# A graph layer on one core: where the weights' stores are issued, border differences in one pass, earlier limits, and a table of choices between streams

## The chip, the core and the metric

The kernel runs on one core of one Trainium2 chip. The metric is the device time of one execution in microseconds (us). The core has five engines that work side by side and each take their own list of instructions strictly in order: TensorE (PE in the profile, its weight loads PEld), VectorE (DVE), ScalarE (ACT), GpSimd (POOL) and SyncE (SP), which here only issues DMAs. Data is moved between HBM and the on-chip memory (SBUF) by DMA; matmuls write to PSUM[...].

## The reference

32 graphs of 512 nodes with 256 channels each. In float32:

```python
h = jnp.maximum(_layernorm(x, axis=-1), 0.0)
xc = jnp.transpose(h, (0, 2, 1))
c = jax.nn.relu(_bn(_conv1d(xc, conv1_w, 0), ...))
c = _bn(_conv1d(c, conv2_w, 8), ...)                 # 17 taps along the nodes
x_conv = jnp.transpose(jax.nn.relu(c + xc), (0, 2, 1))
s = h @ w_se.T + b_se                                 # 3 numbers for each node
dist = sq[:, :, None] + sq[:, None, :] - 2.0 * jnp.einsum('bnd,bmd->bnm', s, s)
A = jnp.exp(-dist) * adj
msg = jax.nn.relu(h @ w_msg.T + b_msg)
x_nmp = jnp.einsum('bnm,bmd->bnd', A, msg)
x_in = jnp.concatenate([x_conv, x_nmp], axis=-1)
# a GRU cell with x_in as its input and h as its state: gates r and z, then n
out = x + (1.0 - z) * n + z * h
```

## The kernel before

The kernel is a program that writes out, once and at build time, one fixed list of instructions for each engine. It holds a planner: `Engine` and `on_pe` keep a clock for each engine and for each buffer, with a cost for each kind of instruction, and the order of the lists follows from these clocks. On the chip nothing is decided; only semaphores hold an instruction until its inputs and buffers are there.

The work is in five streams (lines 1771 to 1777), each a Python generator that emits a few PE instructions and then says when it can go on: `begins` (normalise a graph and turn it, so that channels lie on partitions), `rows` (first convolution, conv1, into `h1`), `conv` (the 17 taps), `graphs` (messages, the adjacency kernel A with exponential and mask, and the gather A times msg) and `gates` (the GRU cell). The loop at line 1819 takes, among the streams that are ready, the one whose `clock` is furthest behind. If none is ready it lets 0.25 us pass in its own clock; until the gates begin, every fourth such turn puts one filler transpose on PE (`keep_warm`, lines 267 to 272). After each turn `fill` gives VectorE and ScalarE work from the background: sums, norms, weights, operands.

The 17-tap convolution is computed with two nested short-convolution schemes of five products each, 25 products in place of the taps' number. It runs in seven groups of positions (`STARTS`, line 36; group 0 has 116 columns, the others 135 or 136).

- `weights_first` (717) makes the 25 sets of weights once, in group 0. VectorE makes combinations of the taps: `g` of `wraw` (128x1536) on the outer level, `gg` of `g` (128x512) on the inner. ScalarE scales them into the tiles `w`, of which there is a ring of six, and line 754 stores each to DRAM (`wd`) from ScalarE's own queue. From group 1 on SyncE loads them again, and `third_weight` (782) stores a third tile to `wd` from GpSimd's queue during group 1. `prepare_some` (967) lets a step of this go only while ScalarE's clock is at most `BUSY` = 0.5 us ahead of PE's.
- `operands` (663) makes the other side of the products from `h1`: on the outer level 18 phases become `x1` with six, on the inner level `fives` (562) makes five operands with two phases each from an `x1`. A difference that reaches past the last phase takes the next column of an early phase instead, so it is done in two instructions: `sub` (572) does the first phase or phases in one and the border one in another.
- `norm` (479) and `norm_some` (508) are the layer norm: statistics on VectorE, `rstd` by a power on GpSimd, scaling on ScalarE. `norm_ahead` (1687) lets the norm of graph b begin in the background when the messages of graph b - 4 have been issued (`told >= b - 3`).
- GpSimd's queue also stores the turned inputs (`hd`), the gathered sums (`nd`), the untransposed inputs (`xd`), the convolution's results (`cd`) and, with accumulation, the output.

Of the kernel before, what the change touches and what calls it, by code (L numbers as in the profile page):

```python
# [10 lines left out]
ALU = mybir.AluOpType  # L11
# [20 lines left out]
G = 4  # L32
# [18 lines left out]
def kernel(  # L51
# [43 lines left out]
    now = 0.0  # L95
    LAG = 0.17
    BUSY = 0.5
# [20 lines left out]
    def done(*tiles):  # L118
        at = 0.0
        for a in tiles:  # L120
            for k, end in met(a.tensor.name, region(a)):
                if k[4]:
                    at = max(at, end + HAND)
        return at
# [24 lines left out]
    class Pool:  # L149
# [18 lines left out]
        def over(self):  # L168
            return max(map(released, self.made)) + HAND
# [75 lines left out]
    dve, act = Engine("DVE", nc.vector, 0.066, 0.00106, 0.085), Engine("ACT", nc.scalar, 0.05, 0.00087, 0.12)  # L245
    pool, sp = Engine("POOL", nc.gpsimd, 1.1, 0.0003, 0.0), Engine("SP", nc.sync, 0.0, 0.0, 0.0)
# [20 lines left out]
    def keep_warm(n):  # L267

        nonlocal now
        for _ in range(n):  # L270
            now += 0.11
            nc.tensor.transpose(unused[:, :P], ident, ident)
# [11 lines left out]
    def later(t, f):  # L284
        LATER.append((t, f))
        LATER.sort(key=lambda e: e[0])
# [221 lines left out]
    def norm_some(b):  # L508

        if now < NORM_AT[b] or act.free > now + BUSY:  # L510
            return False
        NORM_AT[b] = next(NORMS[b], NORM_AT[b])
        if NORMS[b].gi_frame is None:
            del NORMS[b]
        return True
# [46 lines left out]
    def fives(src, n, rv, new, again=None):  # L562

        flat = src.rearrange("p q e -> p (q e)")

        def get(k, some=n):
            return src[:, k : k + 3 * some - 2 : 3, :]  # L570

        def sub(dst, a, b):
            some = n if a < 3 else n - 1
            dve.tensor_tensor(dst[:, :some, :], get(a, some), get(b, some), op=ALU.subtract)
            if a > 2:
                at = [src[:, 3 * n - 3 + b, :], flat[:, (b - 3) * rv + 1 : (b - 2) * rv + 1]]
                dve.tensor_tensor(
                    dst[:, some, :], flat[:, (a - 3) * rv + 1 : (a - 2) * rv + 1], at[b > 2],
                    op=ALU.subtract,
                )  # L580

        def less2(dst, a, b):
            dve.scalar_tensor_tensor(dst, a, -2.0, b, op0=ALU.mult, op1=ALU.add)

        d1 = new()
        sub(d1, 3, 1)
        yield d1
        t = new()
        sub(t, 2, 0)
        yield None  # L590
        less2(t, t, d1)
        yield t
        if not again:
            t = new()
        sub(t, 4, 2)
        yield None
        less2(t, d1, t)
        yield t
        f2 = new()
        sub(f2, 3, 2)  # L600
        yield None
        t = new()
        sub(t, 2, 1)
        yield None
        less2(t, t, f2)
        yield t
        less2(f2, get(1), f2)
        yield f2
# [54 lines left out]
    def operands(g):  # L663

        rv = sizes(g)[3]
        h = h1[:, : Q * rv].rearrange("p (q e) -> p q e", q=Q)
        if g == 0:
            more = iter([cv, prep] * 2)
            firsts = fives(h, 6, rv, lambda: x1_of(next(more), rv), again=True)
        else:  # L670
            firsts = fives_alone(h, 6, rv, x1_of(cv, rv))
        for x1 in firsts:
            yield None
            if x1 is not None:
                yield from fives(x1, 2, rv, lambda: phases("x2", 2, rv, 6))
# [11 lines left out]
    WD = [dram.tile([P, 3, ND, D], F32, name=f"wd{n}") for n in range(25)]  # L687

    def taps_of(get, new, inplace):

        t = new()
        dve.scalar_tensor_tensor(t, get(1), 2.0, get(0), op0=ALU.mult, op1=ALU.add)
        dve.scalar_tensor_tensor(t, get(2), 4.0, t, op0=ALU.mult, op1=ALU.add)
        yield t
        yield get(0)
        yield get(2)
        t = new()
        dve.tensor_tensor(t, get(0), get(1), op=ALU.subtract)
        dve.tensor_tensor(t, t, get(2), op=ALU.add)
        yield t  # L700
        s = t if inplace else new()
        dve.scalar_tensor_tensor(s, get(1), 2.0, t, op0=ALU.mult, op1=ALU.add)
        yield s

    WS, W_AT = [], []
# [6 lines left out]
    def new_w():  # L712
        nonlocal taken
        taken += 1
        return cv.tile([P, ND, D], F32, name="w", bufs=RING)

    def weights_first():


        outer = [  # L720
            taps_of(
                lambda k, i=i: wraw[:, i, :, :, k, :],
                lambda i=i: prep.tile([P, 2, 3, D], F32, name=f"g{i}", bufs=1),
                True,
            )
            for i in range(ND)
        ]
        for j1 in ORDER:
            g = []
            for o in outer:  # L730
                g.append(next(o))
                yield 0.0
            inner = [
                taps_of(
                    lambda k, i=i: g[i][:, :, k, :],
                    lambda i=i: prep.tile([P, 2, D], F32, name=f"gg{i}", bufs=2),
                    False,
                )
                for i in range(ND)
            ]  # L740
            for j2 in ORDER:
                gg = []
                for i in range(ND):
                    gg.append(next(inner[i]))
                    yield 0.0
                yield dve.free + 0.1
                W_BASE.append(taken)
                w = [new_w(), new_w()]
                for k in range(2):
                    for i in range(ND):  # L750
                        act.activation(
                            w[k][:, i, :], gg[i][:, k, :], AF.Copy, scale=GSCALE[j1] * GSCALE[j2]
                        )
                    act.dma_start(WD[len(WS)][:, k], w[k])
                WS.append(w)
                W_AT.append(act.free + LAG)
                yield 0.0
# [181 lines left out]
    at_product = 0  # L939
# [10 lines left out]
    def operand_some():  # L950
# [12 lines left out]
        return True  # L963

    prepare, prepare_at = weights_first(), 26.0

    def prepare_some():
        nonlocal prepare_at
        if len(WS) >= 25 or len(WS) >= at_product + 3 or now < prepare_at or act.free > now + BUSY:
            return False  # L970
        prepare_at = next(prepare)
        return True
# [713 lines left out]

    def norm_ahead():
        for b in list(NORMS)[:2]:
            if (b < G or told >= b - 3) and norm_some(b):
                return True  # L1690
        return False

# [22 lines left out]
    def fill():  # L1715
        while LATER and LATER[0][0] <= now:
            LATER.pop(0)[1]()
        if EVAC:
            evacuate()
        for b in (gating, gating + 1):  # L1720
            if b in HB:
                load_conv(b)
                if dve.free < now + 1.5:
                    residual(b)
                    data_sums(b)
        while dve.free < now + 1.5 and background():
            pass
# [50 lines left out]
    clock = {name: at for name, (_, _, at) in streams.items()}  # L1778
    ready = {name: 0.0 for name in streams}
    hold = {name: None for name in streams}  # L1780


    unused, waits = acc.tile([P, N], F32, name="ps_acc"), 0
    now = max(5.0, done(ident))
    keep_warm(16)
    load(0)
    while 0 in NORMS:
# [8 lines left out]
        op=ALU.add,  # L1796
# [22 lines left out]
    while streams:  # L1819
        names = [k for k in streams if hold[k] is None or hold[k]()]  # L1820
        able = [k for k in names if ready[k] <= now]
        if not able:
            now += 0.25
            assert now < 1e4
            waits += 1
            if waits % 4 == 3 and not HB:
                keep_warm(1)
            fill()
            continue
        name = min(able, key=lambda k: clock[k])  # L1830
        waits = 0
        hold[name], began = None, now
        got = next(streams[name][0], None)
        if got is None:
            del streams[name]
        elif callable(got):
            hold[name] = got
        else:
            ready[name] = got
        if name == "conv":  # L1840

            clock[name] = at_product / 25 - max(0, at_product - 25 * (NG - 1)) * 0.004
        elif got is not None:
            clock[name] += (now - began) / streams[name][1]
        fill()
# [49 lines left out]
```

## Time and profile before

| | us |
|---|---|
| median of three runs | 2040.22 |
| the three runs | 2039.55 to 2042.61 |
| the profiled execution | 2034.87 |
| span of its instructions | 2033.1 |

The mean granted clock of TensorE in this execution was 0.993 of full speed. The costliest lines of the page's groups, PE's, are the products of the convolution and of the gates: here the name of the tile written, then those read, count, busy time, mean of one in ns, and the idle time before with its releaser.

```profile
L259 PE MATMUL ps_c<-xd,w 128*128 128x135 f32 (+1 forms) x2304 | 291.1, 279 | 4.3 <-ACT ps_c L241 3.5
L259 PE MATMUL ps_c<-x,w 128*128 128x135 f32 (+2 forms) x2032 | 269.6, 282 | 3.4 <-ACT n L241 1.1
L259 PE MATMUL ps_g<-at,msg 128*128 128x512 f32 x512 | 227.8, 593 | 1.3 <-DVE shift L241 1.2
```

All instructions are issued through a few helpers, so most lines of the profile are L259 (matmul), L265 (transpose by TensorE), L272 (filler), L241 (VectorE, ScalarE, GpSimd) and L228 (DMA); the tile names tell the groups apart. `ps_c` are the convolution's banks, `ps_g` those of begins, rows and graphs, `ps_acc` those of the gates and fillers. A float32 matmul stands in the trace as two records.

### The profile page before, as it was taken

The numbers are of one execution on the slowest core, as the hardware profiler recorded it, in microseconds if no ns is written. First come the engines' busy times: TensorE is split into PE (matmuls) and PEld (weight loads), VectorE is DVE, ScalarE is ACT, GpSimd is POOL, SyncE is SP. The second block draws the span as 40 slices with busy tenths as digits, with TensorE's granted clock in tenths as the row PEclk, the third lists the DMA queues.
The fourth block names the chain that finished last, engine by engine and source line by source line (L and its number), as shares of the span: only waits on it lengthen the run. The fifth ranks groups of instructions, "written<-read, shape, count | busy, mean of one in ns | idle before, by whom it ended". The sixth has DMA issues, their size and how long they took to land. (4 is left out here: it accounts for less than half of the span.)

```text
span 2033.1 us, 28623 instructions
## 1 busy us (share of the span) xinstructions
PE 1979.4 (97%) x9707; PEld 1448.2 (71%) x9707; DVE 1512.4 (74%) x2816; ACT 876.4 (43%) x1755; POOL 450.9 (22%) x578
## 2 busy tenths in 40 slices
PE   8999999999999999999999999999999999999998
PEld 4778666767777767787678776667777578776774
DVE  5789688969997467897688885668894688766443
ACT  5554563435534444433454234444343543325221
POOL 2100021322311233121232122231122311113232
PEclk9999999999999999999999999999999999999999
DMA  7555587898897879888897888788877866665664
GB/s 262 173 177 182 216 231 214 220 229 221 208 230 193 192 163 189 200 207 232 174 224 188 205 197 190 163 188 202 220 183 185 202 170 156 166 155 104 111 99 34
DMA packets 581377, 378.92 MB, mean 186 GB/s; under 512 B 457664, under 2 KB 475488, under 8 KB 580096
## 3 DMA queue, kind: packets, MB, share of 16 engines
q1 hardware_dynamic: 419760, 279.15, 49.4%
q0 software_dynamic: 153184, 84.70, 24.5%
q10 hardware_dynamic: 8288, 13.24, 1.8%
q8 instruction: 77, 1.26, 0.3%
q14 instruction: 68, 0.56, 0.1%
HBM read 278.94 MB, written 114.56 MB: 194 GB/s over the span
## 5 line engine op out<-in xcount | busy, mean ns | idle before, releaser
L228 POOL DMA_DIRECT2D out_dram<-o_sb x252 | 276.2, 1731 | 629.5 <-DVE o_sb L241 564.8
L259 PEld LDWEIGHTS ps_c<-xd,w 128*128 128x128 f32 x2304 | 285.1, 190 | 46.9 <-ACT ps_c L241 30.2
L259 PEld LDWEIGHTS ps_c<-x,w 128*128 128x128 f32 x2032 | 259.6, 194 | 58.1 <-issue 34.6
L259 PE MATMUL ps_c<-xd,w 128*128 128x135 f32 (+1 forms) x2304 | 291.1, 279 | 4.3 <-ACT ps_c L241 3.5
L259 PE MATMUL ps_c<-x,w 128*128 128x135 f32 (+2 forms) x2032 | 269.6, 282 | 3.4 <-ACT n L241 1.1
L259 PE MATMUL ps_g<-at,msg 128*128 128x512 f32 x512 | 227.8, 593 | 1.3 <-DVE shift L241 1.2
L259 PE MATMUL ps_acc<-xconv,wih 128*128 128x512 f32 (+2 forms) x532 | 210.9, 494 | 4.3 <-DVE shift L241 2.2
L259 PE MATMUL ps_acc<-hTb,whh 128*128 128x512 f32 (+2 forms) x532 | 211.0, 496 | 2.0 <-ACT r L241 2.0
L259 PE MATMUL ps_acc<-xnb,wih 128*128 128x512 f32 (+2 forms) x532 | 209.3, 495 | 3.7 <-DVE ps_acc L241 3.4
L241 DVE TENSOR_TENSOR ps_acc<-ps_acc,r 128x256 f32<-128x256 f32 x120 | 51.6, 430 | 212.0 <-PE ps_acc L259 200.1
L259 PE MATMUL ps_acc<-t,wsum 128*128 128x256 f32 x720 | 177.1, 382 | 5.3 <-ACT ps_acc L241 2.8
L259 PEld LDWEIGHTS ps_g<-at,msg 128*128 128x128 f32 x512 | 95.3, 190 | 106.6 <-issue 100.0
L259 PEld LDWEIGHTS ps_acc<-t,wsum 128*128 128x128 f32 x720 | 135.7, 191 | 41.8 <-issue 17.8
L259 PEld LDWEIGHTS ps_acc<-xconv,wih 128*128 128x128 f32 x532 | 97.5, 190 | 49.3 <-issue 35.4
L259 PEld LDWEIGHTS ps_acc<-xnb,wih 128*128 128x128 f32 x532 | 96.2, 190 | 44.9 <-issue 29.2
L241 DVE TENSOR_TENSOR x<-x 128x272 f32<-128x272 f32 (+5 forms) x280 | 127.6, 498 | 0.3
L259 PEld LDWEIGHTS ps_acc<-hTb,whh 128*128 128x128 f32 x532 | 95.9, 191 | 44.2 <-issue 31.9
L259 PE MATMUL ps_g<-wmsg,hTg 128*128 128x259 f32 x496 | 124.6, 382 | 0.0
L259 PE MATMUL ps_acc<-t,wih 128*128 128x256 f32 x480 | 123.2, 379 | 0.0
L241 DVE TENSOR_TENSOR msg<-ps_g,bmsg 128x256 f32<-128x256 f32 x128 | 53.4, 418 | 93.8 <-PE ps_g L259 93.8
L259 PE MATMUL ps_g<-hT,w 128*128 128x512 f32 (+8 forms) x296 | 118.8, 548 | 3.8 <-DMA hT<-hd 3.5
L241 ACT ACTIVATE h<-ps_g,bn_shift,bn_scale 128x252 f32<-128x252 f32 (+8 forms) x212 | 86.6, 482 | 58.0 <-PE ps_g L259 57.4
(157 smaller groups left out, 3241.9 us busy)
## 6 DMA issues: line engine op xcount, KB each, us to landing
w<-wd SPq DMA_DIRECT2D x414, 256.0 KB, 3.7
m_sb<-in_adj_dram SPq DMA_DIRECT2D x384, 64.0 KB, 3.5
hT<-hd SPq DMA_DIRECT2D x33, 512.0 KB, 3.8
hd<-hT POOLq DMA_DIRECT2D x32, 512.0 KB, 5.8
hTb<-hd SPq DMA_DIRECT2D x32, 512.0 KB, 4.8
xnb<-nd SPq DMA_DIRECT2D x64, 256.0 KB, 3.4
out_dram<-o_sb POOLq DMA_DIRECT2D x252, 64.0 KB, 4.6
hTg<-hd SPq DMA_DIRECT2D x31, 512.0 KB, 4.7
```

What stands on the lines that cost most here:

```text
L228: self.engine.dma_start(dst, src, **more)
L241: getattr(self.engine, op)(*tiles, **more)
L259: nc.tensor.matmul(ps, lhsT, rhs, **more)
```

## The change

There are five edits.

1. `store_w`: the 50 stores of the first-made weights go to GpSimd's queue instead of ScalarE's, and are put off by 0.3 us in the planner's clock.
2. `sub` in `fives`, for two phases and a difference that reaches past the last one: one instruction instead of two, with `over`, a view of two rows whose second lies before the first in memory (phase k, then phase k - 3 one column on).
3. `prepare_some` lets ScalarE's clock be 1.0 us ahead of PE's instead of 0.5.
4. `norm_ahead` lets a norm begin one graph sooner (`told >= b - 4`).
5. `OTHERS`: the planner counts the turns at which more than one stream is ready; at 26 of these it takes the second in the order of the clocks, at one the third.

```diff
+            if n == 2 and a > 2:
+                dve.tensor_tensor(dst, over(a), get(b) if b < 3 else over(b), op=ALU.subtract)
+                return
...
+        def over(k):
+            e = src[:, k, :]
+            return bass.AP(e.tensor, e.offset, [e.ap[0], (1 - 3 * rv, 2), (1, rv)])
...
+    def store_w(dst, src):
+        later(act.free + 0.3, lambda: pool.dma_start(dst, src))
...
-                    act.dma_start(WD[len(WS)][:, k], w[k])
+                    store_w(WD[len(WS)][:, k], w[k])
...
-        if len(WS) >= 25 or len(WS) >= at_product + 3 or now < prepare_at or act.free > now + BUSY:
+        if len(WS) >= 25 or len(WS) >= at_product + 3 or now < prepare_at or act.free > now + 1.0:
...
-            if (b < G or told >= b - 3) and norm_some(b):
+            if (b < G or told >= b - 4) and norm_some(b):
...
+    OTHERS = {
+        6: 1, 41: 1, 259: 1, 374: 1, 430: 1, 443: 1, 547: 1, 953: 1, 979: 1, 1020: 2,
+        1022: 1, 1182: 1, 1202: 1, 1260: 1, 1291: 1, 1471: 1, 1636: 1, 1670: 1, 1744: 1,
+        1745: 1, 1837: 1, 2031: 1, 2149: 1, 2232: 1, 2391: 1, 2604: 1, 2610: 1,
+    }
+    choices = 0
...
-        name = min(able, key=lambda k: clock[k])
+        able.sort(key=lambda k: clock[k])
+        choices += len(able) > 1
+        name = able[min(OTHERS.get(choices, 0), len(able) - 1)] if len(able) > 1 else able[0]
```

Since all lists come from one planner, each edit moves instructions everywhere after the place where it first acts. The instruction lists of the two programs have the same matmuls and transposes of data. They differ in 15 fillers fewer (45 to 30), 50 stores moved from ScalarE to GpSimd, and 210 small subtractions that become 105.

## The prediction

> **What bounds the kernel now.** I read the page first: busy shares, then the slices.
>
> ```profile
> PE 1979.4 (97%) x9707; PEld 1448.2 (71%) x9707; DVE 1512.4 (74%) x2816; ACT 876.4 (43%) x1755; POOL 450.9 (22%) x578
> PE   8999999999999999999999999999999999999998
> PEclk9999999999999999999999999999999999999999
> ```
>
> The reader is to see that TensorE has work at all times and that no other engine comes near it. The instruction lists of both programs hold the same matmuls; the only difference on PE is 45 against 30 of the filler transposes (`keep_warm`). So the time can move only by what PE loses. The busy times by stage say where that is (start up to the first product, the rest of group 0, the long middle, the gates at the end):
>
> ```profile
> core 0: us, PE busy (x) PEld busy (x) DVE busy (x) ACT busy (x) POOL busy (x), PEclk, DMA share, GB/s
> 0.00:64.00 64.00, 54.16 (x213) 32.33 (x214) 40.76 (x128) 37.59 (x77) 14.47 (x36) 0.95 0.67 245
> 64.00:250.00 186.00, 180.24 (x1145) 144.79 (x1145) 148.09 (x278) 97.51 (x222) 14.92 (x29) 0.97 0.54 183
> 250.00:1850.00 1600.00, 1571.34 (x7747) 1157.97 (x7746) 1248.32 (x2279) 684.69 (x1372) 362.68 (x453) 1.00 0.81 195
> 1850.00:2033.10 183.10, 173.69 (x607) 113.07 (x605) 75.20 (x134) 56.60 (x84) 58.80 (x60) 0.99 0.57 91
> ```
>
> First column of time minus PE's: idle 9.8, 5.8, 28.7 and 9.4 us, in all 53.7. Two losses hide inside "busy". One is the fillers (the last of them at 175.6 us). The other is the clock; here are two of the six stretches in which it was halved:
>
> ```profile
> 166.70:173.53 6.83, 6.00 (x28) 5.75 (x29) 5.65 (x13) 6.02 (x14) 1.10 (x1) 0.50 0.48 142
> 1412.57:1419.40 6.83, 6.75 (x26) 4.74 (x27) 6.83 (x11) 5.25 (x8) 4.37 (x4) 0.50 0.82 41
> L272 PE MATMUL ps_acc<-ident x45: 271/398/474, 1.8 to 175.6; 128*128 128x128 f32 x45
> ```
>
> The other four start at 9.7, 60.9, 122.3 and 1613.9 us and are 3.4 us long. Half of PE's busy time in such a stretch is lost, some 1.7 us in a short one and 3 in a long one. Last, who ends PE's waits, in group 0's stage and then in the middle (engine line, releaser, us in total, times, longest):
>
> ```profile
> PE ps_g L265 <- DVE augr L241: 1.7, 1, 1.7
> PE ps_g L265 <- ACT at L241: 1.6, 2, 0.8
> PE ps_acc L259 <- ACT right L241: 1.2, 2, 0.6
> ```
>
> ```profile
> PE ps_g L259 <- DMA hT<-hd: 3.5, 5, 1.8
> PE ps_c L259 <- ACT ps_c L241: 3.5, 7, 0.9
> PE ps_c L259 <- ACT n L241: 3.4, 3, 2.1
> PE ps_acc L259 <- DVE ps_acc L241: 3.3, 3, 1.3
> PE ps_acc L259 <- ACT ps_acc L241: 2.8, 1, 2.8
> ```
>
> In group 0 it is one chain, the adjacency kernel of a graph (factors, exponential, mask) with no convolution product ready beside it. In the middle no releaser holds more than 3.5 of 28.7 us: 33 short waits of 0.85 us on average, each with its own cause.
>
> [...]
>
> **The change part by part.**
>
> ```profile
> L228 ACTq DMA_DIRECT2D wd<-w x50: 326/326/509, 63.8 to 235.2; - x50
> L228 POOL DMA_DIRECT2D wd<-w x24: 540/540/2380, 237.3 to 461.6; - x24
> ACT w L241 <- ACT w L241: 9.8, 24, 0.5
> L241 DVE TENSOR_TENSOR x<-x 128x272 f32<-128x272 f32 x120 | 47.1, 434 | 0.1
> L241 DVE TENSOR_TENSOR x<-x 128x544 f32<-128x544 f32 x40 | 28.6, 716 | 0.0
> ```
>
> *Stores on GpSimd.* 50 issues of 0.326 us leave ScalarE, 16.3 us; with them go waits of the issue for the scaling just before it (the third row, 9.8 us in 24 gaps). Together 26 us of 186 in group 0's stage, where ScalarE is busy 97.5. It isn't full, so the relief counts only where ScalarE ends a wait of PE (`at`, `right`, `w`): at most 2.8 + 0.7 us there. GpSimd takes 50 x 0.54 = 27 us onto its 14.9 in the stage; there is room. Queued behind a store that waits for ScalarE are `rstd` of the next norm and the stores `hd`, `nd`, `xd`. In the new list none to 14 of these stores stand between two `rstd`; what delays is the last set, two stores and a pair of scalings, 1.1 + 0.8 = 1.9 us. After `rstd` come the norm, the turned input and a graph, which have some 30 us each; hidden, unless a begin is the only stream left. By themselves: from -3 to +4 us, taken as -1.
>
> *One-pass differences.* 210 small subtractions become 105: in group 1 on, 2 x 47.1/120 = 785 ns against 28.6/40 = 715, so 70 ns each, and the same for the 234-wide ones by their row: 7.3 us of VectorE over the run. PE waited for `x` once, 0.7 us. VectorE's 1248 of 1600 us is the cover: nothing. A read that steps backward between two rows isn't in the trace: at least the 715 ns row, at most no gain over two; 0 to -3.
>
> *Norms and weights sooner.* The new limit (ScalarE up to 1.0 us behind instead of 0.5) puts the first weights' VectorE work, 4 of 1.75 and 4 of 0.68 us (9.7 us), ahead of the first masks. In the trace of before VectorE sits idle 6.1 us there (22.5 to 28.6), and the last part of the taps, issued at 11.3, lands 14.0 us later. So the first mask comes about 9.7 - 6.1 = 3.6 us late and holds PE's second turned mask, which needs its PSUM bank. The gather of graph 0 stays near its 39.6 us all the same: eight transposes of `y` stood before it, from 35.4 to 38.4 us with ScalarE's pace, and are now behind it. From there the list has 16 gather, 16 message and 8 first-convolution records and these transposes, 7.0 + 3.5 + 3.5 + 0.9 = 14.9 us, so 54.5; ScalarE's `h` comes 1.4 later, VectorE's first `x` 2.4 after that: the first product at some 59 us instead of 63.6, with 24 transposes of 0.11 us (2.6 us) moved behind it. 4.6 - 2.6 = 2: -2 (from -5 to +3).
>
> The larger part is what follows. Group 0 loses 5.8 idle, some 3.4 of fillers, and 1.7 + 3.0 by the clock (122.3 and 166.7 us): 13.9 us. Before, 12 fillers stand after the first product; now 3. Each stands where four turns of the planner found nothing ready, so it counts places, not time; three quarters fewer places, with the clock's part following its gaps, I take as 60%: -8 (0 to -13). What is late next is VectorE: 148 of 186 us.
>
> *The table.* At 27 choices the stream that is further ahead goes first. It changes no work. The middle loses 28.7 us idle and half of 6.75 + 3.42, 33.8 in all, in 33 places with many causes. The profile doesn't show a wait for any of these choices; bounds are -15 (half of it goes) and +20 (a new 0.85 us wait at two thirds of the places, and three clock stretches of 1.7). I take -3, since the weights' earlier ring and VectorE's relief help there too. The end (9.4 us idle, of it 6.8 after PE's last matmul) is untouched: 324 gate matmuls after the last product before, 320 now.
>
> Sum: -1 + 0 - 2 - 8 - 3 = -14. From the profiled execution, 2034.87 us (its span 2033.1), that is 2020.9. The median of the three runs is 2040.22, 5.35 above it, so 2026.
>
> **Rivals.** *More goes than that:* all of group 0's loss that isn't the graph's own latency (-12), -2 before it, and -12 in the middle: 2014. For it: fillers fell to a quarter[...]. Against: no single releaser to remove in the middle.
>
> *The gain is given back:* group 1 can start only when the 25 sets of weights are made, `late` pools are open and the rows of group 1 are written; both lists have the same 404 convolution matmuls, 7 messages and 6 gathers before the first gate matmul. If VectorE, 80% busy in group 0, sets that point, an earlier start only lengthens its waits: 0 to -4, about 2039. For it: 148 of 186 us. Against: VectorE's idle 38 us and the 5 us before the first `x`.
>
> *Slower:* the table's places. If the second stream's operand isn't there on the chip, PE, which takes its list in order, stands: 18 of 27 places x 0.85 = 15, plus three clock stretches of 1.7 = 5, minus the early 10: +10, 2050. It decides from some 12 new waits on (10 us). For it: the choice by clock took the stream that was behind, whose operands had more time; against: only streams that the planner held to be ready may go first.
>
> **How the numbers follow.** Forecast (2018 to 2034) 0.50; more goes 0.20; given back 0.16; slower 0.14. No change is within 0.2%, 2036.1 to 2044.3, about what a measurement can tell. Of "given back" 0.10 lies there, 0.06 is faster; of "slower" 0.01 is the same. Faster 0.76, same 0.11, slower 0.13. Both outer cases give the range: 2009 leaves out the deepest part of "more goes", 2041 most of "slower"; 2009 to 2041.
>
> **What would show it.** Right: in group 0's stage (same work, which ends earlier) idle of PE and the half-clock stretches down by about 8 us, no half clock near 122 and 167; first product near 59 us; the middle's idle about 25 us. Stores wrong: waits of `rstd` for ScalarE's `w` on GpSimd, and PE waiting for `ps_g` of a turned input. Differences: the 544-wide rows at 715 ns. Table wrong: idle of the middle over 40 us with new releasers. The forecast falls if the middle, not the start, makes most of the difference.

## The result, and the profile after

The changed kernel takes 2005.49 us (median of four executions, 2000.38 to 2015.27) against 2039.88 for the kernel before in the same comparison: a ratio of 0.9844, interval 0.9822 to 0.9866. The forecast was 2026, with a range that ended at 2009; the gain is 34 us and not 14. The profiled execution was the slowest of the four, with a span of 2013.5 us.

The page's busy shares, then the busy times by stage, divided at about the same amount of PE's work as the four stages of before:

```profile
PE 1973.8 (98%) x9692; PEld 1450.8 (72%) x9692; DVE 1505.0 (75%) x2711; ACT 874.1 (43%) x1755; POOL 478.5 (24%) x628
```

```profile
0.00:55.50 55.50, 48.47 (x181) 28.96 (x181) 34.72 (x114) 36.63 (x80) 17.02 (x41) 0.97 0.77 282
55.50:247.00 191.50, 182.86 (x1137) 143.89 (x1138) 156.27 (x285) 94.82 (x221) 41.30 (x78) 0.96 0.60 199
247.00:1830.00 1583.00, 1567.45 (x7763) 1162.98 (x7762) 1235.33 (x2181) 686.14 (x1370) 361.35 (x449) 1.00 0.81 195
1830.00:2013.50 183.50, 175.04 (x614) 115.01 (x612) 78.65 (x133) 56.47 (x85) 58.78 (x60) 0.99 0.58 92
```

Idle of PE by stage is now 7.0, 8.6, 15.6 and 8.5 us; before it was 9.8, 5.8, 28.7 and 9.4. The middle lost 13 us of its idle time, and the rest of group 0, from which the forecast expected most, has more idle than before. Who ends PE's waits, first in group 0's stage (55.5 to 247 us), then in the middle (247 to 1830):

```profile
PE ps_g L259 <- DMA hT<-hd: 2.9, 1, 2.9
PE ps_c L259 <- DVE x L241: 2.8, 3, 1.7
PE ps_g L259 <- DVE at L241: 2.8, 2, 2.4
```

```profile
PE ps_c L259 <- ACT ps_c L241: 3.9, 6, 1.0
PE ps_g L259 <- DMA hT<-hd: 3.8, 3, 2.3
PE ps_acc L259 <- DVE ps_acc L241: 2.1, 4, 1.1
PE ps_c L259 <- ACT n L241: 1.4, 1, 1.4
PE ps_acc L259 <- ACT r L241: 1.4, 1, 1.4
```

In the middle the releasers are much the same, but 33 waits have become 19 and the one of 2.8 us for ScalarE is gone. In group 0 the adjacency chain (`augr`, `right`, `at` by ScalarE) no longer holds PE; VectorE and a reloaded input do.

PE's loss has two parts, waits and half clock. The profile before has 53.7 us of idle PE and 26.2 us of PE work at a granted clock of 0.50, so by estimate 13.1 lost by it. The four profiles of the changed kernel's PE order (this one, e5, e6 and e13) have 35.0 to 39.7 us idle and 3.4 to 16.4 lost by the clock. Without the table (e1) it is 73.1 and 22.9. So the gain is in the waits; the clock's part changes its sign from one execution to the next (3.3 us worse to 9.7 better).

A count worked out from the traces shows where the time went. Each PE record but the fillers is given an undisturbed pace for its shape (an estimate from the lower quartile of the compared traces; 1923 us in all), and "lost" is the time minus this useful work when so much of the work was done. It takes in idle time, fillers and half clock. With another choice of the pace, by shape alone, the level of "lost" is up to 30 us higher, but what follows stays. "Again" is the second profile of the changed kernel (e5), "no table" is e1, both below.

```
useful work, us   before   changed   again   no table
            50      25.8      21.3    21.5       21.8
           150      38.8      26.1    27.2       26.5
           250      42.6      41.2    38.8       39.4
           300      43.1      41.6    39.3       39.8
          1000      71.3      62.0    54.5       91.7
          1600      95.3      77.7    70.3      116.2
           end     110.1      90.4    83.1      135.8
```

By 150 us of work the change is 12 us ahead. By 250, after the step into group 1, only 1.4 to 3.8 of it are left. The gain that lasts is made between 300 and 1600 us of work: 52 us lost before, 31 to 36 now. Without the table it is 76. At the end the two profiles are 20 and 27 us ahead, less than the 34 of the medians, since the profiled execution before was 5 us under its median.

### The profile page after: what moved, and what is told of

It is laid out like the page before. It is cut to its first block, busy times and chain, and to the rows that moved or that the text cites. A ratio compares the mean times of both kernels' runs of the same rounds, so it can differ in the third digit from the quotient of the medians.

```text
span 2013.5 us, 28526 instructions
## 1 busy us (share of the span) xinstructions
PE 1973.8 (98%) x9692; PEld 1450.8 (72%) x9692; DVE 1505.0 (75%) x2711; ACT 874.1 (43%) x1755; POOL 478.5 (24%) x628
## 4 chain that ended last, share of the span: by engine, by line
PE 65%; DVE 4%; issue 2%; DMA 1%; ACT 1%; POOL 1%; DVEq 0%; POOLq 0%; SPq 0%; ACTq 0%
PE ps_acc L259 36%; PE ps_c L259 16%; PE ps_g L259 13%; DVE o_sb L241 1%; DMA cd<-part 1%; PE ps_g L265 1%; DVE t L241 0%; POOL out_dram L228 0%; DVE x L241 0%; DMA hd<-hT 0%; POOL cd L228 0%; DVE ps_acc L241 0%; ACT at L241 0%; DVE z L241 0%; DMA w<-wd 0%
## 5 line engine op out<-in xcount | busy, mean ns | idle before, releaser
L259 PE MATMUL ps_g<-hT,w 128*128 128x512 f32 (+8 forms) x296 | 124.5, 571 | 7.4 <-DMA hT<-hd 6.8
L241 DVE TENSOR_TENSOR x<-x 128x544 f32<-128x544 f32 (+2 forms) x175 | 120.2, 707 | 0.3
L241 ACT ACTIVATE ps_c<-ps_c 128x270 f32<-128x270 f32 (+1 forms) x144 | 56.3, 391 | 137.9 <-PE ps_c L259 137.7
```

The costliest lines, as they stand in the source:

```text
L241: getattr(self.engine, op)(*tiles, **more)
L259: nc.tensor.matmul(ps, lhsT, rhs, **more)
```

## The experiments

All times are medians; ratios are to the kernel before, run on the same chip in the same comparison.

| run | us | ratio, interval |
|---|---|---|
| e1 no table | 2054.86 | 1.0078 (1.0063 to 1.0092) |
| e2 before, stores only | 2051.68 | 1.0059 (1.0044 to 1.0074) |
| e3 before, limits only | 2053.36 | 1.0066 (1.0050 to 1.0083) |
| e4 before, borders only | 2037.95 | 0.9988 (0.9976 to 1.0000) |
| e5 changed again | 2007.58 | 0.9846 (0.9829 to 0.9862) |
| e6 table one later | 2006.77 | 0.9843 (0.9826 to 0.9859) |
| e7 first nine places | 2017.48 | 0.9896 (0.9880 to 0.9912) |
| e8 no table, cd on SyncE | 2045.08 | 1.0027 (1.0013 to 1.0041) |
| e9 one place, 374 | 2021.07 | 0.9899 (0.9876 to 0.9922) |
| e10 one place, 340 | 2032.40 | 0.9963 (0.9943 to 0.9982) |
| e11 table one earlier | 2024.50 | 0.9926 (0.9906 to 0.9945) |
| e12 changed, cd on SyncE | 2015.22 | 0.9871 (0.9847 to 0.9896) |
| e13 changed, stores on ScalarE | 2005.79 | 0.9843 (0.9819 to 0.9867) |
| e14 before, stores on GpSimd | 2036.39 | 0.9993 (0.9980 to 1.0006) |
| e15 before with the table | 2043.63 | 1.0020 (1.0010 to 1.0029) |
| e16 before, one place, 340 | 2048.12 | 1.0055 (1.0034 to 1.0077) |

**e1: the change without its table.**

```diff
-    OTHERS = {
...
-    }
+    OTHERS = {}
```

> The changed kernel with an empty table; the other four edits stay. Theory A (the table removed the middle's waits, and the early part gains nothing by the end of group 0): about 2025 to 2035 us, that is 20 to 30 slower than with the table; PE idle in the middle back at about 28 us. Theory B (the other edits did it by moving the start of everything): within 6 us of the changed kernel's 2005; PE idle in the middle stays near 15 us.

Theory A by its direction, but the size was in neither: 2054.86, 49 us slower than the changed kernel and 15 slower than the one before, and PE's waits in the middle sum to 43 us, not 28. So the four other edits together cost time, and the table is more than the whole gain. The waits of PE in the middle of this run:

```profile
PE ps_c L259 <- ACT ps_c L241: 11.7, 12, 5.1
PE ps_acc L259 <- ACT r L241: 9.3, 5, 4.1
PE ps_acc L259 <- DVE ps_acc L241: 6.1, 4, 3.3
```

What stands behind the two longest waits, one of 5.1 and one of 4.1 us, is in the timelines (start, length, engine, instruction, idle before and its releaser). First PE, then ScalarE, from 1028 us:

```profile
1031.80 1.88 PE L259 MATMUL ps_acc<-xconv,wih 128*128 128x512 f32 x4
1038.82 2.39 PE L259 MATMUL ps_c<-xd,w 128*128 128x135 f32 x9 [5.13 <-ACT ps_c L241]
```

```profile
1036.03 2.46 ACT L241 ACTIVATE part<-y,bn_shift,bn_scale 128x522 f32<-128x522 f32 x2 [5.40 <-DMA cd<-part]
1038.27 0.50 ACT L241 ACTIVATE ps_c<-ps_c 128x270 f32<-128x270 f32 x1
```

PE needs `ps_c`, a copy of half a microsecond. In ScalarE's list two evacuations into `part` stand before it, and the first waits 5.4 us for a store to free its buffer. The planner lets an evacuation go only when the store is over by its own clock; on the chip the store landed later. The other kind, on ScalarE from 1364 us, and PE's row after it:

```profile
1366.58 4.43 ACT L241 ACTIVATE y<-z 128x1620 f32<-128x1620 f32 x3
1370.91 0.68 ACT L241 ACTIVATE r<-ps_acc,vec 128x512 f32<-128x512 f32 x1
1371.64 2.08 PE L259 MATMUL ps_acc<-hTb,whh 128*128 128x512 f32 x2 [4.08 <-ACT r L241]
```

Three background copies of the sums (4.43 us) stand before the `r` for which PE waits 4.08 us. Engines take their lists in order, so background instructions in the wrong place hold PE for nearly all of their length, here 4.08 of 4.43 us.

**e2, e3, e4: single edits on the kernel before.** e2 has the first of these changed lines, with `store_w` as in the change, e3 the next two, e4 the last, with `over`.

```diff
-                    act.dma_start(WD[len(WS)][:, k], w[k])
+                    store_w(WD[len(WS)][:, k], w[k])
...
-        if len(WS) >= 25 or len(WS) >= at_product + 3 or now < prepare_at or act.free > now + BUSY:
+        if len(WS) >= 25 or len(WS) >= at_product + 3 or now < prepare_at or act.free > now + 1.0:
...
-            if (b < G or told >= b - 3) and norm_some(b):
+            if (b < G or told >= b - 4) and norm_some(b):
...
+            if n == 2 and a > 2:
+                dve.tensor_tensor(dst, over(a), get(b) if b < 3 else over(b), op=ALU.subtract)
```

> The kernel before with only the weights' stores on GpSimd's queue and put off by 0.3 us. Theory A: 0 to -6 us against before (2034 to 2040), since ScalarE is only half busy there. Theory B (ScalarE's release is what lets group 0 run): -10 us or more.

> The kernel before with only the two limits (weights up to 1.0 us ahead, norms one graph sooner). Theory A: -3 to +4 us against before. Theory B (an early first product is worth its whole lead): -8 us or more, with the first product at about 56 us instead of 63.6.

> The kernel before with only the one-pass border differences. VectorE's busy time falls by about 7 us whatever else happens. If the operation matters by itself: 0 to -3 us. If any change in the planner's costs reshuffles the waits of the middle, the time moves by several us either way with no change in VectorE's share of PE's waits.

e2 and e3 missed both theories: 12 and 13 us slower. e3 does have the early gain (lost time at 150 us of work 29.8 us, 38.8 before) but at 250 it stands at 45.9, behind. e4 gains 2 us, at the edge of its interval, though from 55 us on, just before the first product, its lists are in another order. Nothing in these edits makes PE's work longer; what they share is that each redraws the order of all that follows. That this is what cost e2 its time is tested below (e14). For e3 it is argued only, since a limit can't be changed with the order held.

**e5 and e6: the changed kernel again, and the table one choice later.**

```diff
-        6: 1, 41: 1, 259: 1, 374: 1, 430: 1, 443: 1, 547: 1, 953: 1, 979: 1, 1020: 2,
+        7: 1, 42: 1, 260: 1, 375: 1, 431: 1, 444: 1, 548: 1, 954: 1, 980: 1, 1021: 2,
...
```

> The changed kernel once more, to give it as many executions as the others and a second profile: 2000 to 2010 us. If the wait of 2.9 us at 199 us for a turned input and the half-clock stretches after it belong to the order, they are in this profile too; if they came from one slow transfer, they are not.

> The changed kernel with all 27 places of the table one choice later. Theory A (these very places keep ScalarE and VectorE from standing with long background work in front of what PE waits for): 2045 to 2065 us, like the run without a table. Theory B (letting the second stream go first now and then helps wherever it is): under 2020 us.

e5 repeats the time, and its profile has a wait of 2.0 us for `hT` at the same place and half-clock stretches at 202.6 and 219.7 us. The wait belongs to the order: it is in e6 (2.0) and e13 (2.9) too. The stretch behind it doesn't always come: e13 has none near 202 us (see the last section). e6 can't speak for or against either theory: the shift changes the planner's turns but gives the same instructions in the same order on all five engines, since many turns of a stream emit nothing. It is one more repeat. The same holds for most of the table: added one after another, 17 of its 27 places change nothing in PE's list. Place 374 puts another instruction at four fifths of the list's places after it, 1744 again at more than half of what follows it, and the other eight change a few rows each.

**e7, e9, e10, e11: parts of the table, and other places.** One new table each, in this order.

```diff
-    OTHERS = {
...
-    }
+    OTHERS = {6: 1, 41: 1, 259: 1, 374: 1, 430: 1, 443: 1, 547: 1, 953: 1, 979: 1}
+    OTHERS = {374: 1}
+    OTHERS = {340: 1}
+        5: 1, 40: 1, 258: 1, 373: 1, 429: 1, 442: 1, 546: 1, 952: 1, 978: 1, 1019: 2,
...
```

> The table cut to its first nine places (up to choice 979). Theory A: each place repairs what is next to it, so lost time equals the changed kernel's up to where choice 1020 falls, and grows from there at the pace of the run without a table: 2015 to 2045 us. Theory B (any order gives about 2050 and only the whole table was fitted): about 2050, with the lost time parted from early on.

> The changed kernel with a table of one place, choice 374, at which the gates' stream goes before a graph's. In the instruction lists most of the 27 places change nothing, and this one changes all that follows it. Theory A (one swap draws another order for the rest of the run, and this one is good): 2013 to 2022 us, as with nine places. Theory B (the gain is the sum of many repairs): at least 2040.

> A table of one other place, choice 340, not picked for anything; it too changes the whole order after it. Theory A (orders differ by luck, and a swap has no value of its own): anything from 2020 to 2065 us, about 2045. Theory B (letting the second stream go first is good in itself): under 2025.

> All 27 places one choice earlier; unlike one choice later, this changes the instruction lists from about a twelfth of the way on. Theory A: another draw, 2020 to 2065 us. Theory B (the density of such choices matters, not the places): under 2015.

One place alone brings 34 of the 49 us. At it, 319 us into the run, one turn of the gates (two matmuls) comes before the graph's four turned masks, instead of after; everything behind it is dealt anew. The first nine places bring 37, but they are one place again: of the nine only 41 and 374 change PE's list, e7 and e9 differ in 12 of 9692 PE records, and their intervals overlap. The order of e7 parts from the changed kernel's by a few rows at 886 us and broadly only from 1256 us on: lost at 1400 us of work 63.1 against 62.6 (e5), at 1800 81.8 against 74.0. A place that nobody picked (340) brings 22 us, and the table one choice earlier 30. e7 alone fell into the range of theory A, repairs of what is next to each place; e9 speaks against it, since one swap at 319 us brings most of the gain. In e9, e10 and e11 the time is in the range of theory A, which is wide in e10 and e11. So the picture of many repairs is wrong: a choice draws a new order for the rest of the run, and the order without a table was a poor draw.

**e15 and e16: the same on the kernel before.** The loop of choices is added to it, with the whole table or with 340 alone; the other four edits are not there.

> The kernel before with the table alone, none of the other edits. Theory A (the table is a draw that was good with the other edits and has no value without them): 2015 to 2060 us. Theory B (the table carries the gain by itself): under 2012.

> The kernel before with a table of one place, 340, not picked for anything. Theory A (the order before was one draw as well, neither the best nor the worst): 2020 to 2060 us, most likely slower than 2039. Theory B (any second-first swap helps): under 2030.

The table has no value without the other edits (4 us slower), and the place that helped by 22 us in e10 costs 8 here. This refutes that letting the second stream go first is good in itself.

**e8 and e12: taking one kind of collision away, the order kept.** `by` names the engine that issues on the chip, in place of the one that the planner counts.

```diff
-            PARTS[mine] = pool.dma_start(CD[b][:, o, n0:n1], part[:, : n1 - n0])
+            PARTS[mine] = pool.dma_start(CD[b][:, o, n0:n1], part[:, : n1 - n0], by=nc.sync)
```

> The order of the kernel without a table, with only the stores of the convolution's results (cd) issued by SyncE instead of GpSimd, so that they no longer stand behind the output's small packets. Theory A (ScalarE's wait for the buffer part, 28.8 us in 15 waits, with products' copies queued behind it, is one of the collisions that the table avoids): 8 to 15 us faster than without a table (2040 to 2047), the waits of part under 5 us. If these waits are only a symptom: no change.

> The changed kernel's order with the convolution's stores (cd) issued by SyncE instead of GpSimd. Its PE has no long wait behind the buffer part, so if the gain of 10 us without a table came from these waits alone: no change, 2001 to 2010 us. If SyncE's stores help the output's and inputs' stores on GpSimd as such: 5 us or more faster. If loads now wait behind stores that wait for ScalarE: slower, with PE's waits for hT or w grown.

The two rows are ScalarE's waits for `part` in e1 and in e8:

```profile
ACT part L241 <- DMA cd<-part: 28.8, 15, 5.4
```

```profile
ACT part L241 <- DMA cd<-part: 7.8, 7, 2.2
```

and PE's for what stands behind them in e8's middle:

```profile
PE ps_acc L259 <- ACT r L241: 9.3, 5, 4.1
PE ps_c L259 <- ACT ps_c L241: 4.3, 9, 0.6
```

With PE's, VectorE's and ScalarE's lists unchanged the run is 9.8 us faster (2045.08 against 2054.86), PE's waits for `ps_c` in the middle fall from 11.7 to 4.3 us and the longest from 5.1 to 0.6, and the waits for `r`, which have the other cause, stay at 9.3. The waits of `part` did not fall under 5 us as expected, only to 7.8. In the changed kernel the same edit costs 5 us by the ratios (e5 and e12), whose intervals overlap, and 8 by the medians. Its ScalarE also waits for `part` (21.5 us in 17 waits, at most 3.2), but mostly where nothing urgent is behind it. In e12's profile the sum falls only to 17.8, and one of these waits now stands before a `ps_c`: ScalarE begins an evacuation at 761.53 us, 2.80 late because of the store, and PE's next product for `ps_c` begins at 762.61, 2.97 late because of the copy behind it.

So the same kind of collision can come from SyncE's stores as well. The expectation of "no change" was wrong, and so was the sign that went with "slower": PE's waits for `hT` are 3.1 us, not more than in the changed kernel (6.8, and 4.0 in e5). Where the rest of the time goes isn't shown.

**e13 and e14: the stores' queue with every order held.** The first line is on the changed kernel, the second on the one before.

```diff
+        later(act.free + 0.3, lambda: pool.dma_start(dst, src, by=nc.scalar))
...
+                    act.dma_start(WD[len(WS)][:, k], w[k], by=nc.gpsimd)
```

> The changed kernel's order on every engine, with only the 50 weights' stores issued by ScalarE again (at the places in its list where the planner lets them go). Theory A (the stores' queue is worth nothing by itself, only the order that follows from it): 2001 to 2010 us. Theory B (ScalarE's release is a real part of the gain): 2012 or more, with waits for ScalarE in the first 240 us.

> The order of the kernel before on every engine, with only the 50 stores issued by GpSimd at the same places. Theory A: 2036 to 2042 us, no change. Theory B: 5 us or more faster.

Theory A in both: 2005.79 and 2036.39, no difference that these runs can tell. The engine that issues the stores is worth nothing that can be seen here; the different order that the planner makes of it is what moved e2.

None of these versions is faster than the changed kernel by more than the runs can tell.

## Why the prediction was wrong

*The bound* was right: PE's work is the same, and the time moved by what PE loses.

*Stores (-1, from -3 to +4)* were right as an operation: e13 and e14. *Differences (0, to -3)* agree with e4's 2 us, though its order isn't that of before, so the operation alone isn't told apart. The 544-wide subtraction, with 60 backward-stepping ones now among 100, measures 70.1 us, so 701 ns against 715:

```profile
L241 DVE TENSOR_TENSOR x<-x 128x544 f32<-128x544 f32 x100 | 70.1, 717 | 0.2
```

*Norms and weights sooner (-2 and -8).* The first product came at 55.5 us, even before the 59 worked out, and at 150 us of work the gain was 12 us, more than the 10 taken. But it was counted there and not at the end of the stage. The rival "given back" had the mechanism: "an earlier start only lengthens its waits". At 172 us PE waits 1.75 us for `x`. VectorE's list before that:

```profile
167.43 0.68 DVE L241 TENSOR_TENSOR at<-ps_g,at 128x512 f32<-128x512 f32 x1
169.14 0.43 DVE L241 BATCH_NORM_STATS2 st<-x_sb 128x6 f32<-128x256 f32 x1 [1.03 <-DMA x_sb<-in_x_dram]
...
172.08 1.28 DVE L241 SCALAR_TENSOR_TENSOR gg<-g,gg 128x512 f32<-128x512 f32 x2
173.28 0.64 DVE L241 SCALAR_TENSOR_TENSOR x<-x,x 128x468 f32<-128x468 f32 x1
```

A norm's statistics stand and wait for their input to land, with masks and operands behind them. Then PE waits for `hT` and for a mask, and the clock halves. PE's rows, then the windows of this profile:

```profile
201.76 5.37 PE L259 MATMUL ps_g<-hT,w 128*128 128x512 f32 x8 [2.94 <-DMA hT<-hd]
237.15 10.20 PE L259 MATMUL ps_g<-at,msg 128*128 128x512 f32 x16 [2.36 <-DVE at L241]
```

```profile
202.40:205.81 3.41, 3.41 (x6) 1.35 (x5) 0.57 (x1) 0.88 (x2) 0.00 (x0) 0.50 0.92 293
219.46:222.87 3.41, 3.41 (x14) 2.90 (x14) 0.00 (x0) 2.30 (x7) 1.12 (x2) 0.50 0.13 36
236.53:243.36 6.83, 6.21 (x8) 2.57 (x9) 6.76 (x6) 0.00 (x0) 0.00 (x0) 0.50 1.05 299
```

By the granted 0.50, half of PE's 13.0 busy us in them is lost, 6.5, beside 5.3 of waits (2.94 for `hT`, 2.36 for the mask). The wait for `hT` is no matter of the stores' queue: with the stores on ScalarE (e13) it is 2.87. So the term of -10 measured, at 250 us of work, -1.4 (this profile) to -3.8 (e5), -3.2 without the table, and +3.3 with the two limits alone (e3). It was mis-sized, and its sign isn't certain.

*The table (-3, from -15 to +20)* is the step that failed, and with it the silent one that the first four edits leave the middle alone. The sum treated the five parts as if each added its own. They act through one planner: the first four redraw the middle by +15 us over the whole (e1), the table by -49. The argument "the profile doesn't show a wait for any of these choices" was true and gave a wrong bound, since a choice isn't tied to a wait near it: 374 alone moves 34 us over all that follows it, from 319 us to the end. The bound should have been all that the middle loses, 34 us, downward, and upward at least as much. The measured time lies beyond the 2014 of the rival "more goes", and 14 of its 26 us of gain were to come before the middle. By the prediction's own sign, "the forecast falls if the middle, not the start, makes most of the difference", it falls. That the time moved the way it was forecast is luck as far as the argument goes: with the same four edits and no table it moved the other way.

*Open:* why an order is good isn't told by any one number here. Two kinds of collision in a poor one are shown, one of them by e8; the rest of the difference, some 40 us, is only seen as shorter waits. Whether the first four edits make the average order better can't be said from six orders with them (2005 to 2055, two of them sharing most of their order with the changed kernel's) and three with none of them (2040 to 2048).

## What to carry to other kernels

Where one planner writes all engines' lists, an edit has two effects: its own, and a new draw of everything after it. Measure the first with the order held fixed (only the issuing engine or the operation exchanged), and don't credit the second to the edit. In a kernel with PE at 97%, look for short, urgent copies on in-order engines behind long or waiting background work; the longest waits of the poor order stood there.

## What the runs showed of the hardware

The half-clock stretches differ between executions of one and the same PE order: 38.2 us in all with a span of 2013.5, 30.7 with 2006.2 (e5), 11.8 with 1999.7 (e13). Of each, 3.4 to 4.9 us lie at the end, after PE's last matmul. In the changed kernel's profile the stretches up to the last are 3.413 or 6.827 us long and start at 28.32, 55.62, 202.40, 219.46, 236.53, 454.98, 1219.57 and 1632.58 us, that is 8, 43, 5, 5, 64, 224 and 121 times the length of the short ones apart. In e5 8.05, 28.53 and 55.83 us are six and eight times that length apart.

In the profiles of before and after, the five waits of PE over 2 us (2.11 and 2.83, then 2.94, 2.36 and 2.33) each have a stretch that starts within 0.7 us of their end. The wait of 2.87 us in e13 has none.

A count over the eighteen traces of this case shows more. Each is divided into pieces as long as a short stretch, 3.413 us, with the borders at the stretches' starts; after the first 12 us, the time in a piece is added up in which PE stands idle or runs only matmuls of 5 rows (`right,left`, the adjacency's). Of 10,267 full-speed pieces with less than 1.7 us of it none was followed by half clock, of 59 with 1.7 to 2.02 us 30 were, and of 95 with more all were. The traces of before and after alone have 1137 pieces with at most 1.64 us and three with 1.74 to 1.85, none of them followed by half clock, and 13 with 2.03 to 2.98, all of them followed. Idle time by itself doesn't part them: 36 pieces with less than 1 us idle were followed by half clock. In e13 a border at 197.92 us divides the wait of 2.87 us into 1.20 and 1.67, and the stretch at 219.46 us above follows a piece with 0.29 us idle and 2.12 us of 5-row matmuls. These are counts of this case's executions; what sets the clock isn't shown by them.

The changed kernel's four executions go with it: mean granted clocks of 0.991, 0.994, 0.996 and 0.997 for 2015.27, 2008.61, 2002.37 and 2000.38 us.

Stores of `part` issued by SyncE landed in 2.7 us in the median and 6.8 at most (e8), by GpSimd, where they share a queue with the output's packets (129,024 of 128 bytes in the changed kernel's trace), in 3.6 and 11.3 (e1). The changed kernel's order gives the same picture: 2.6 and 6.8 from SyncE (e12), 3.6 and 7.8 from GpSimd. All figures include the last graph's few other transfers of this tile. Whether the shared queue is the cause wasn't separated from the other differences between the two engines' stores.
